# A mixture-of-experts layer on one core: two experts' first-layer rows loaded one block at a time, GpSimd's router sums ahead of two weight combinations, and the logits' additions split off

## The chip, the cores and the metric

The kernel runs on one core of a Trainium2 chip. A core has TensorE (PE, matrix products into the eight PSUM banks), VectorE (DVE, elementwise work and reductions), ScalarE (ACT, activations and copies), GpSimd (POOL, elementwise work in SBUF and its own DMA queue) and SyncE (SP, here only a DMA queue). The engines run side by side, each takes its instructions in program order, and they wait for one another on semaphores. The time is the device time of one execution, in microseconds (us). Before the change it is 463.31 us, the median of three runs (463.06 to 463.71).

## The reference

For 8 sequences of 512 tokens with 256 features each, all in float32:

```
nx       = layer_norm(x)
weights  = softmax(nx Wq (ctx Wk)^T / 16)          # 64 context rows per sequence
evidence = weights (ctx Wv)
combined = [nx, evidence, cond]                    # 768 features
probs    = softmax(combined router_W + router_b)   # 3 experts
h_e      = silu(combined e_w1[e] + e_b1[e])        # 512 wide, e = 0, 1, 2
routed   = sum_e probs_e (h_e e_w2[e] + e_b2[e])
g        = sigmoid(silu(combined gate_w1 + gate_b1) gate_w2 + gate_b2)
out      = x + g (routed out_w + out_b)
```

## The kernel before

**Pairs and products.** The sequences are worked on two at a time, so there are four pairs j = 0 to 3. Matrix products over a pair are done with seven products instead of eight, so weights and activations are first combined by a few subtractions and additions. `combine_weights(g)` does this for expert g's first layer (g = 3, that is E, is the gate): four GpSimd instructions (L248 to L251) read the first two blocks of the weight tile `w1`, write sums into `ws`, and one of them (L250) writes back into `w1`. `combine_gate` does the same for the gate's second layer.

**Weights.** `load_first(g, part)` loads 256 rows of expert g's first weights into `w1`, as two blocks of 128 rows, with one DMA on SP's queue. Part 0 (the rows for nx) of experts 1 and 2 is issued late, after the anchors' rows. The tile `w1` holds its four blocks one behind the other in each partition, each block with the columns of all three experts and the gate, so one expert's two blocks are two stretches with other experts' columns between them.

**The first pair.** The setup is part of the run, and the first pair has its own list of slots, `SLOTS_0`. In each slot two half products (64 of 128 rows each) run side by side on TensorE; after the bar stand the steps that other engines do, in the order in which they are issued. All engines follow program order here. A step `k` copies a partial sum out of PSUM (ACT), `a` and `w11.0` add one (DVE, L878), `s` is the silu (ACT, L872). `lp0.0` to `lp1.3` are `router_part`: a multiply with a running sum over one quarter of a sequence (DVE, L636), and after a sequence's fourth one, eight small GpSimd copies (L643) that spread the sums into the logits' tile `lg`. `c2` is `combine_weights(2)` and `cg` is `combine_gate`. `rl` is `router_logits`: two products with their sums (L749, L752), then four small operations on `lg` (L755 to L761). `rx` is the exponential (ACT, with a table load on both sides), `r` the normalisation and the spreading of the probabilities by DMA, `g0` a subtraction for the gate (L1222), `st` the layer norm's statistics of the next pair (L579, L580), `lx`, `l1` and `l2` loads of the next pair's x and of second-layer weights. `weigh_chunk` (L915, L912) multiplies the hidden values by the probabilities. After the slots come six units of second-layer weights (`transpose_second` on DVE, L531; `second_layer` on TensorE, L541).

**Before the slots.** `end_softmax` issues on GpSimd, in this order: `combine_weights(0)`, `router_column` (which makes `gg`, the vector of `router_part`; L414, L415), the DMAs of the router's bias and rows (L419, L435), `combine_weights(1)`. `end_setup` ends with `second_bias`, four small DVE operations on `b2o` (L562 to L567), which is read only in `outputs`.

**The pairs after.** Pairs 1 to 3 use the list `SLOTS`; their router is worked in `outputs` of the pair before.

Of the kernel before, what the change touches and what calls it, by code (L numbers as in the profile page):

```python
# [8 lines left out]
F32 = mybir.dt.float32  # L9
# [7 lines left out]
def kernel(  # L17
# [51 lines left out]
    nc = tc.nc  # L69
# [87 lines left out]
    def rows_of(w):  # L157
        return w.rearrange("(k p) n -> p k n", p=P)
# [74 lines left out]
    def load_first(g, part):  # L233
        src, n = (e_w1[g], RH) if g < E else (gate_w1, H)
        lo = part * KH
        nc.sync.dma_start(
            w1[:, lo : lo + KH, g * RH : g * RH + n], rows_of(src[part * H : (part + 1) * H, :])
        )

    def load_anchor(g):  # L240
        src = e_w1[g] if g < E else gate_w1
# [499 lines left out]
                w[side(i, h), 1 - h, :, :].rearrange("p j c -> p (j c)"),  # L741
            )

    def router_logits(j):
        w, lg, vr = S["w", j], S["lg", j], S["vr", j]
        le = work.tile([P, ED, NJ], F32, tag="le", name=f"le_{j}")
        for e in range(ED):
            pv = work.tile([P, 2, NJ, TB], F32, tag="pv", name=f"pv_{j}_{e}", bufs=1)
            nc.vector.tensor_tensor(  # L749
                pv, w, vr[:, e, :, :].unsqueeze(2).to_broadcast([P, 2, NJ, TB]), ALU.mult  # L750
            )
            nc.vector.tensor_reduce(  # L752
                le[:, e, :], pv.rearrange("p g j c -> p j g c"), AX.XY, ALU.add
            )
        nc.vector.tensor_tensor(  # L755
            lg[:, 1:, :], lg[:, 1:, :], rbias[:, j, :].unsqueeze(2).to_broadcast([P, ED, NJ]), ALU.add
        )
        nc.vector.tensor_tensor(lg[:, 1:, :], le, lg[:, 1:, :], ALU.add)
        mx = work.tile([P, NJ], F32, tag="rmx", name=f"rmx_{j}")
        nc.vector.tensor_reduce(mx, lg.rearrange("p e j -> p j e"), AX.X, ALU.max)  # L760
        nc.vector.tensor_tensor(  # L761
            lg, lg, mx.unsqueeze(1).to_broadcast([P, E, NJ]), ALU.subtract
        )

    def router_exp(j):
        S["ex", j] = work.tile([P, E, NJ], F32, tag="ex", name=f"ex_{j}")
        nc.scalar.activation(S["ex", j], S.pop(("lg", j)), AF.Exp)
# [149 lines left out]
    def gate_layer(j, steps):  # L917
# [101 lines left out]
        "P1.3 P1.1 | lp0.0 a10.0",  # L1019
        "Y.0 W.0 | k00.1 lp0.1 s10.0 lp0.2",  # L1020
        "P2.1 P1.3 | w11.0",
        "P4.0 P5.1 | a00.0 k00.3 s11.0 lp0.3 c2",
        "P6.1 P2.1 | lp1.0 s00.0 lp1.1",
        "P5.1 Z.2 | a00.1",
        "U.0 P6.1 | lp1.2 k11.1 lp1.3 cg lx l1 l2 s00.1",
        "P1.2 P5.2 | rl k10.1",
        "Y.2 P4.0 |",
        "P5.2 P1.2 | s01.0",
        "P2.3 P3.1 | k00.2 k11.2",
        "P7.1 V.1 | g0 rx",  # L1030
        "P2.2 Z.3 | st0.0 st0.1",
        "P6.2 P7.1 | st0.2 st0.3",
# [57 lines left out]
    def half_layers(j):  # L1090
# [23 lines left out]
        def half(token, k):  # L1114
# [17 lines left out]
            "xb0": lambda: load_x_blocks(2 * j),  # L1132
            "xb1": lambda: load_x_blocks(2 * j + 1),
            **{f"g{n}": lambda n=n: gate_differences(j, (n,)) for n in range(4)},
            "rl": lambda: router_logits(j),
            "rx": lambda: router_exp(j),
            "c2": lambda: combine_weights(2),
            "cg": lambda: combine_gate(),
            "lx": lambda: [load_x(b) for b in (2, 3)],
# [277 lines left out]
    with tc.manual_schedule(engines=None):  # L1417
        ctx_rows = context.flatten_outer_dims().rearrange("(t p) d -> p t d", p=P)
        for d in range(2):
            half = slice(d * NX // 2, (d + 1) * NX // 2)  # L1420
            nc.sync.dma_start(ctx_sb[:, half, :], ctx_rows[:, half, :])
        for w_sb, w in ((wk_sb, Wk), (wq_sb, Wq)):
            nc.scalar.dma_start(w_sb, rows_of(w))
        for dst, src in late_rows:
            nc.scalar.dma_start(dst, src)
        nc.sync.dma_start(wv_sb, rows_of(Wv))
        load_table(AF.Sqrt)
        load_x(0)
        load_x(1)
        load_first(E, 1)  # L1430
        load_first(E, 0)
        load_anchor(E)
        load_first(0, 1)
        load_first(0, 0)
        load_first(1, 1)
        load_first(2, 1)
        load_anchor(0)

        wake(7)
        context_transposes()  # L1440
        transpose_weights(wkT, wk_sb, "wk")
        transpose_weights(wqT, wq_sb, "wq")
        statistics(0, 0, NT)
        deviation(0, 0)
        normalize(0)
        project(wv_sb, ctxT, keep_v, "v", (0,))
        join_keys()
        project(wv_sb, ctxT, keep_v, "v", (1,))
        statistics(1, 0, NT // 2)
        small_transposes()  # L1450
        statistics(1, NT // 2, NT)
        combine_weights(E)
        transpose_x(0)
        late_scratch()
        load_anchor(1)
        load_anchor(2)
        nc.sync.dma_start(ow_sb, rows_of(out_w))
        load_first(1, 0)
        load_first(2, 0)
        nc.sync.dma_start(gw2_sb, rows_of(gate_w2))  # L1460
        load_second(0)
        deviation(0, 1)
        load_router_column()
        normalize(1)
        project(wkqT, ctxT, keep_m, "m")
        transpose_x(1)
        value_weights(0, E)
        router_anchor()
        anchor_rows(E)
        store_router_rows(0)  # L1470
        store_router_anchor()
        load_table(AF.Exp)
        combine_x(0, nc.vector, (0, 1))
        spares(6, 4, 5, 7)
        scores(0)

        def begin_softmax():
            exponents(0)
            combine_x(0, nc.vector, (2,))

        def end_softmax():
            sum_weights(0)
            softmax(0)
            nc.gpsimd.tensor_copy(wake_t, S["w", 0][:, 0, 0, 0:1])
            value_differences(0, 0)
            turn_weights(0)
            anchor_columns(E)
            combine_x(0, nc.vector, (3,))
            combine_weights(0)
            router_column()  # L1490
            spread_router_bias()
            spread_router_rows(0)
            combine_weights(1)

        def end_setup():
            value_differences(0, 1)
            late_anchors()
            for g in range(E):
                anchor_columns(g)
            value_differences(0, 2)  # L1500
            second_bias()

        for j in range(NP):


            within, between = {}, {}

            def put(where, n, step, *args):
                where.setdefault(n, []).append(lambda: step(*args))

            spares(7, 5)
            if j == 0:
                spares(4, 5, 7)
                copies = []

                def value_product(g):
                    value_weights(0, g, lambda *args: copies.append(args), False)

                def copy_values():
                    nc.scalar.copy(*copies.pop(0))  # L1520

                put(within, 1, value_product, 0)
                put(within, 1, begin_softmax)
                put(within, 5, copy_values)
                put(within, 6, load_table, AF.Silu)
                put(within, 3, value_product, 1)
                put(within, 3, copy_values)
                put(within, "sums", end_softmax)
                put(within, 7, value_product, 2)
                put(within, 7, copy_values)  # L1530
                put(within, 7, end_setup)
            else:
                put(within, 3, value_weights, j, 1, nc.scalar.copy, False)
            if j + 1 < NP:
                b0, b1 = 2 * j + 2, 2 * j + 3
                if j + 2 < NP:
                    put(between, "begin", load_x, b0 + 2)
                    put(between, "begin", load_x, b1 + 2)
                put(between, "begin", transpose_blocks, b0)
                put(between, "gate", regroup_x, b1)  # L1540
                put(between, "begin", value_weights, j + 1, E)
                put(between, "begin", store_router_rows, j + 1)
                put(between, "begin", spread_router_rows, j + 1)
                put(between, "P5", transpose_blocks, b1)
                put(between, "P6", value_weights, j + 1, 2)
                put(between, "P2", scores, j + 1)
                put(between, "P2", exponents, j + 1)
                put(between, "P2", combine_x, j + 1, nc.gpsimd)
                put(between, "P7", softmax, j + 1)
                put(between, "P7", value_weights, j + 1, 0)  # L1550
                put(between, "P7", router_logits, j + 1)
                put(between, "P3", turn_weights, j + 1)
                put(between, "P3", router_exp, j + 1)
            gate_layer(j, within)
            half_layers(j)
            outputs(j, between)

# [33 lines left out]
```

## Time and profile before

| | |
|---|---|
| median of three runs | 463.31 us (463.06 to 463.71) |
| profiled execution, its time | 463.15 us |
| profiled execution, its span | 460.8 us (granted clock 0.991) |
| PE busy | 452.3 us (98%) |
| DVE busy | 364.4 us (79%) |
| ACT busy | 214.1 us (46%) |
| POOL busy | 99.5 us (22%) |
| DMA moved | 35.31 MB, mean 77 GB/s |

The span is what the trace covers; the profiled execution's time is 2.3 us longer. Times "at 50.1" below are microseconds from the start of the span. A row of the timeline gives start, duration, engine, line, operation and tiles, and in brackets how long the engine had been idle before it and what released it. In a table of windows each engine's busy time in a stretch is given, then PEclk, the granted share of TensorE's clock. The first pair's slots run from 33.2 to 89.1, its second-layer units from 89.1 to 99.6.

### The profile page before, as it was taken

How to read it: one execution, taken by the hardware profiler on the slowest of the kernel's cores; microseconds unless marked ns; L12 is line 12 of the kernel's file. 1: busy time of each engine (PE TensorE's matmuls, PEld its weight loads, DVE VectorE, ACT ScalarE, POOL GpSimd, SP SyncE). 2: the span in 40 equal slices, each digit the busy share in tenths (PEclk: the TensorE clock that was granted, in tenths of full speed). 3: DMA queues.
4: the chain of work that ended last, by engine and by line, in shares of the span. 5: the costliest groups of instructions: out<-in, count | busy, mean ns of one | idle time of the engine just before them, and what ended most of it. 6: DMA issues, size and time to landing. Idle time of an engine off the chain costs nothing.

```text
span 460.8 us, 5500 instructions
## 1 busy us (share of the span) xinstructions
PE 452.3 (98%) x1797; PEld 217.2 (47%) x1797; DVE 364.4 (79%) x683; ACT 214.1 (46%) x373; POOL 99.5 (22%) x148
## 2 busy tenths in 40 slices
PE   9999699999999999999999999999999999999996
PEld 7544355574444444444444444444444444444445
DVE  2879699967779999578869999678969846677983
ACT  3545485457220476468220476558130456558000
POOL 5429600081053400001044300001044300000010
PEclk9999899999999999999999999999999999999999
DMA  8983664362011368402011357202011381000014
GB/s 265 384 165 92 110 195 80 48 137 46 7 23 23 47 216 133 111 0 46 8 23 23 47 189 143 37 0 46 7 23 23 47 208 23 1 0 0 1 16 75
DMA packets 119348, 35.31 MB, mean 77 GB/s; under 512 B 105981, under 2 KB 116281, under 8 KB 118809
## 3 DMA queue, kind: packets, MB, share of 16 engines
q1 hardware_dynamic: 115312, 27.02, 28.9%
q0 software_dynamic: 2080, 7.16, 4.6%
q10 hardware_dynamic: 1928, 0.80, 0.7%
q8 instruction: 14, 0.23, 0.2%
q14 instruction: 14, 0.11, 0.1%
HBM read 27.56 MB, written 7.39 MB: 76 GB/s over the span
## 4 chain that ended last, share of the span: by engine, by line
PE 87%; DMA 6%; POOL 3%; DVE 1%; issue 1%; SPq 0%; DVEq 0%; POOLq 0%
PE ps_u L836 42%; PE ps_z L836 19%; PE ps_y L836 12%; DMA w<-in_L_xcond_e_w_dram 5%; PE ps_vw L811 4%; PE ps_gu L836 3%; PE ps_w2o L541 2%; PE ps_gz L836 1%; DMA x<-in_x_dram 1%; PE ps_s L685 1%; PE ps_tokens L836 1%; POOL lg L643 1%; PE ps_gy L836 1%; POOL ws L249 1%; POOL ws L248 0%
## 5 line engine op out<-in xcount | busy, mean ns | idle before, releaser
L836 PE MATMUL ps_u<-nxT,w 64*128 64x512 f32 (+1 forms) x208 | 97.4, 595 | 0.0
L915 DVE TENSOR_TENSOR h<-h,pb 128x512 f32<-128x512 f32 x96 | 64.3, 701 | 16.2 <-ACT h L872 12.5
L836 PE MATMUL ps_u<-h,w2o 128*128 128x512 f32 x144 | 64.2, 595 | 0.0
L872 ACT ACTIVATE h<-h,abias 128x512 f32<-128x512 f32 x72 | 49.3, 718 | 29.4 <-DVE h L878 29.4
L836 PE MATMUL ps_y<-nxT,w 64*128 64x512 f32 (+1 forms) x104 | 53.3, 609 | 0.0
L836 PE MATMUL ps_z<-nxT,ws 64*128 64x512 f32 (+1 forms) x104 | 53.1, 599 | 0.0
L836 PE MATMUL ps_z<-wT,vw 64*128 64x512 f32 x104 | 52.3, 590 | 0.0
L836 PE MATMUL ps_z<-T,ws 64*128 64x512 f32 (+1 forms) x104 | 50.5, 589 | 0.0
L836 PEld LDWEIGHTS ps_u<-nxT,w 64*128 64x128 f32 (+1 forms) x208 | 37.6, 190 | 26.4 <-issue 23.8
L1322 POOL TENSOR_TENSOR yb<-yb,xb 128x512 f32<-128x512 f32 x14 | 17.7, 1266 | 148.8 <-DVE yb L1321 131.7
L836 PE MATMUL ps_u<-T,ws 64*128 64x512 f32 (+1 forms) x104 | 49.5, 598 | 0.0
L836 PE MATMUL ps_u<-T,w 64*128 64x512 f32 x112 | 48.5, 589 | 0.0
L836 PE MATMUL ps_z<-h,w2s 128*128 128x512 f32 x96 | 42.5, 592 | 0.0
L836 PEld LDWEIGHTS ps_u<-h,w2o 128*128 128x128 f32 x144 | 27.0, 190 | 32.6 <-issue 30.8
L881 ACT COPY h<-ps_u 128x512 f32<-128x512 f32 x48 | 27.7, 580 | 24.9 <-PE ps_u L836 24.9
L1289 DVE TENSOR_TENSOR h<-h,h 128x1024 f32<-128x1024 f32 x24 | 34.3, 1486 | 0.0
L836 PE MATMUL ps_u<-wT,vw 64*128 64x512 f32 x56 | 29.1, 609 | 3.8 <-DVE h L878 3.8
L427 POOL DMA_DIRECT2D vrd<-vw x8 | 5.0, 628 | 114.2 <-ACT vw L818 111.6
L836 PEld LDWEIGHTS ps_z<-h,w2s 128*128 128x128 f32 x96 | 18.2, 190 | 22.9 <-issue 22.2
L836 PE MATMUL ps_y<-wT,vw 64*128 64x512 f32 x56 | 28.3, 595 | 0.0
L811 PE MATMUL ps_vw<-w,vT 128*128 128x512 f32 (+1 forms) x64 | 26.7, 539 | 0.0
L836 PEld LDWEIGHTS ps_z<-nxT,ws 64*128 64x128 f32 (+1 forms) x104 | 19.9, 192 | 13.4 <-issue 10.8
(230 smaller groups left out, 822.2 us busy)
## 6 DMA issues: line engine op xcount, KB each, us to landing
pb<-pd POOLq DMA_DIRECT2D x4, 1536.0 KB, 6.6
xb<-in_x_dram SPq DMA_DIRECT2D x64, 64.0 KB, 2.5
out_dram<-yb SPq DMA_DIRECT2D x56, 64.0 KB, 2.0
w<-in_L_xcond_e_w_dram SPq DMA_DIRECT2D x6, 512.0 KB, 11.8
x<-in_x_dram SPq DMA_DIRECT2D x24, 128.0 KB, 3.0
xd<-x SPq DMA_DIRECT2D x24, 128.0 KB, 2.4
xg<-xd SPq DMA_DIRECT2D x48, 64.0 KB, 2.3
scr_wa<-in_L_xcond_e_w_dram SPq DMA_DIRECT2D x3, 512.0 KB, 9.3
```

What stands on the lines that cost most here:

```text
L249: add(s2, s1, a11, ALU.subtract)
L427: nc.gpsimd.dma_start(S["vrd", j][i].rearrange("e c -> c e"), S["vw", j][row_half(i), R0:])
L541: nc.tensor.matmul(ps[:, d * H : (d + 1) * H], w2["T"][u % 2][:, c : c + P], ow_sb[:, k, :], start=(k == 0), stop=(k == KH - 1),)
L643: nc.gpsimd.tensor_copy(lg[side(a, h), 2, q::NT], sums[q * TB : (q + 1) * TB, 2 * h : 2 * h + 2])
L685: nc.tensor.matmul(ps[side(i, h), g * NH : (g + 1) * NH], mr[:, k, 2 * j + i, g * TB : (g + 1) * TB], S["nxT", 2 * j + i][:, k, h * NH : ( ...
L811: nc.tensor.matmul(ps, vT[:, k, j * 2 * CT : (j + 1) * 2 * CT], w1[:, KH + k, n0:n1], start=(k == 0), stop=(k == KH - 1),)
L836: return nc.tensor.matmul(ps, lhsT, rhs, start=start, stop=True, skip_group_check=not start)
L872: nc.scalar.activation(h, h if src is None else src, AF.Silu, bias=abias[:, c, 2 * j + i : 2 * j + i + 1])
L881: nc.scalar.copy(chunk(n, i, d), part)
L915: nc.vector.tensor_tensor(h, h, S["pb", j][:, i, :, 2 * q // RC, :], ALU.mult)
L1289: nc.vector.tensor_tensor(d, p, m, ALU.subtract)
L1322: nc.gpsimd.tensor_tensor(yb, yb, S["xb", 2 * j + row][:, i, :], ALU.add)
```

## The change

Four things are changed, all of which touch the first pair alone in what runs when:

- `load_first` loads part 0 of experts 1 and 2 with two DMAs, one for each block of 128 rows, instead of one. SP's queue has two DMAs more (265 instead of 263).
- In `SLOTS_0`, `c2` goes from the sixth slot to the ninth, behind `lp1.3`, `l1` and `l2`, and `cg` goes behind it. On GpSimd the eight copies of the second sequence now stand before `combine_weights(2)`; the two combinations follow each other.
- `router_logits` is split. `evidence_logits` (the step `rl`, where it was) holds the two products with their sums. `router_logits` (the step `rs`) holds the four small operations on `lg`, three slots later, behind `k11.2`. For the later pairs the two are issued one behind the other, as before.
- `second_bias` leaves `end_setup` and becomes the step `b2`, two slots ahead of `rs`.

```diff
     def load_first(g, part):
         src, n = (e_w1[g], RH) if g < E else (gate_w1, H)
         lo = part * KH
-        nc.sync.dma_start(
-            w1[:, lo : lo + KH, g * RH : g * RH + n], rows_of(src[part * H : (part + 1) * H, :])
-        )
+        for k in range(KH) if g in (1, 2) and not part else (slice(0, KH),):
+            nc.sync.dma_start(
+                w1[:, lo : lo + KH, g * RH : g * RH + n][:, k],
+                rows_of(src[part * H : (part + 1) * H, :])[:, k],
+            )
...
-    def router_logits(j):
-        w, lg, vr = S["w", j], S["lg", j], S["vr", j]
-        le = work.tile([P, ED, NJ], F32, tag="le", name=f"le_{j}")
+    def evidence_logits(j):
+        w, vr = S["w", j], S["vr", j]
+        S["le", j] = le = work.tile([P, ED, NJ], F32, tag="le", name=f"le_{j}")
         for e in range(ED):
...
+
+    def router_logits(j):
+        lg, le = S["lg", j], S.pop(("le", j))
         nc.vector.tensor_tensor(
             lg[:, 1:, :], lg[:, 1:, :], rbias[:, j, :].unsqueeze(2).to_broadcast([P, ED, NJ]), ALU.add
         )
...
-        "P4.0 P5.1 | a00.0 k00.3 s11.0 lp0.3 c2",
+        "P4.0 P5.1 | a00.0 k00.3 s11.0 lp0.3",
         "P6.1 P2.1 | lp1.0 s00.0 lp1.1",
         "P5.1 Z.2 | a00.1",
-        "U.0 P6.1 | lp1.2 k11.1 lp1.3 cg lx l1 l2 s00.1",
+        "U.0 P6.1 | lp1.2 k11.1 lp1.3 lx l1 l2 c2 cg s00.1",
         "P1.2 P5.2 | rl k10.1",
-        "Y.2 P4.0 |",
+        "Y.2 P4.0 | b2",
         "P5.2 P1.2 | s01.0",
-        "P2.3 P3.1 | k00.2 k11.2",
+        "P2.3 P3.1 | k00.2 k11.2 rs",
         "P7.1 V.1 | g0 rx",
...
-            "rl": lambda: router_logits(j),
+            "rl": lambda: evidence_logits(j),
+            "rs": lambda: router_logits(j),
             "rx": lambda: router_exp(j),
+            "b2": lambda: second_bias(),
...
             value_differences(0, 2)
-            second_bias()
...
+                put(between, "P7", evidence_logits, j + 1)
                 put(between, "P7", router_logits, j + 1)
```

## The prediction

> **What bounds the kernel now.** I read the engines' shares first, then the page's 40 slices.
>
> ```profile
> PE 452.3 (98%) x1797; PEld 217.2 (47%) x1797; DVE 364.4 (79%) x683; ACT 214.1 (46%) x373; POOL 99.5 (22%) x148
> PE   9999699999999999999999999999999999999996
> DVE  2879699967779999578869999678969846677983
> PEclk9999899999999999999999999999999999999999
> ```
>
> TensorE is the bound in 38 of 40 slices. Only the fifth slice (46.1 to 57.6 us) has a hole in its middle, and there the granted clock dips too; the last slice is the drain at the end. So a change to the first pair is worth what it does to that hole. Next, who waits for whom, on PE and on DVE:
>
> ```profile
> PE ps_u L836 <- DVE h L878: 3.8, 1, 3.8
> DVE lg L755 <- POOL lg L643: 3.0, 1, 3.0
> ```
>
> PE waits once, 3.8 us, for an addition on DVE; shortly before, DVE waits 3.0 us for GpSimd's router copies. The chain that ended last gives the links in time (start, length):
>
> ```profile
> 15.45 16.69 DMA w<-in_L_xcond_e_w_dram
> 32.29 0.64 POOL ws L248
> 44.84 0.65 POOL ws L248
> 49.71 0.19 DVE lg L755
> 53.72 0.70 DVE h L878
> 54.46 1.22 PE ps_u L836
> ```
>
> GpSimd is held until a weight DMA lands at 32.14, is then busy without a break, finishes the second sequence's copies at 49.7, DVE does its logits, one gate subtraction (L1222) and four statistics, then `a11.1` (53.72), which releases PE. GpSimd's own timeline shows the queue:
>
> ```profile
> 32.29 0.63 POOL L248 TENSOR_TENSOR ws<-w 128x256 f32<-128x256 f32 x1 [5.70 <-DMA w<-in_L_xcond_e_w_dram]
> 41.98 2.78 POOL L643 COPY lg<-ls 32x2 f32<-32x2 f32 x8
> 47.25 0.63 POOL L251 TENSOR_TENSOR ws<-w,ws 128x256 f32<-128x256 f32 x1
> 47.95 1.73 POOL L643 COPY lg<-ls 32x2 f32<-32x2 f32 x8
> ```
>
> The windows add the second half of the loss (after the stretch: its length, then each engine's busy time, then the clock):
>
> ```profile
> 49.70:54.40 4.70, 0.98 (x6) 0.15 (x2) 4.25 (x15) 2.79 (x3) 2.27 (x4) 0.85 0.75 120
> 54.40:60.00 5.60, 5.54 (x14) 2.87 (x16) 5.36 (x18) 4.16 (x7) 2.70 (x6) 0.51 0.16 24
> 70.00:80.00 10.00, 10.00 (x49) 5.26 (x47) 9.86 (x28) 5.57 (x9) 0.00 (x0) 1.00 0.40 69
> ```
>
> After the hole PE runs at half clock. Half products, 0.43 us apart before, follow at 0.86 us from 54.46 to 59.74: 5.3 us for 2.65 us of work. The hole itself is 3.95 us (next start due at 50.51, came at 54.46). Together 6.6 us of PE's time. In the third window DVE is the full engine: what DVE has gained by 54 us limits what PE can keep.
>
> **The change, part by part.** The sum is made against the profiled execution: 463.15 us, span 460.8, 2.3 around it; it lies 0.16 under the median of 463.31.
>
> *Block loads.* Expert 0's combination reads columns of `w1`, which one load of experts 1 or 2, seen as a stretch from its first to its last column, spans. In the built order its first instruction waits for two of SP's DMA lanes before, and for one after; the lane left is also that of expert 0's own load, issued at 8.5 and landed by 15.4. So GpSimd need not wait until 32.14 but starts behind `wake_t` at 26.6, 5.7 us earlier. Then 2.7 us for expert 0, 1.6 for `gg`, 2.1 for four DMA issues, 3.4 for expert 1 (its blocks landed by 30.3 as one load, wanted now at 33.1): free at about 36.4, before 42.0. The four block DMAs carry the same bytes in the same place; the two more issues, 0.47 us each, are hidden in SP's idle time between 35.3 and 40.7, ahead of the x loads, whose start DVE sets. Without that cover: 0.9 us on x, which lands at 44.9 now and is read at 48.
>
> *Copies ahead of the combinations.* The second sequence's copies need only DVE's last `lp1.3`, about 42.4 in the new order, so they end about 43.8. DVE reaches the logits at about 46.5. Its 2.97 us wait is gone. What is late next: `combine_weights(2)` ends about 46.7, 1.2 us before its 47.9, so being put behind costs nothing; PE's first reader of those sums, P6.6, comes ten slots behind the hole, at about 59. The gate's combination ends about 49 instead of 52.1, read at 99.6.
>
> *`second_bias` and the split.* The four `b2o` operations (1.18 us from 36.07 to 37.25) move behind the evidence sums. They still stand ahead of `a11.1`, so its chain does not get shorter; the `lp` steps get 1.2 us earlier. The split moves four small operations (1.0 us) three slots on. Both cost nothing more; neither removes work.
>
> *DVE's chain.* From 33.38 to `a11.1` at 53.72 are 20.34 us, with 2.97 us of waiting. The same instructions stand in it afterwards: 33.38 + 17.37 = 50.75. Durations shift where GpSimd moves:
>
> ```profile
> 40.70 0.83 DVE L636 SCALAR_TENSOR_TENSOR junk<-x,gg 128x256 f32<-128x256 f32 x1
> 41.57 0.74 DVE L636 SCALAR_TENSOR_TENSOR junk<-x,gg 128x256 f32<-128x256 f32 x1
> 43.33 0.43 DVE L636 SCALAR_TENSOR_TENSOR junk<-x,gg 128x256 f32<-128x256 f32 x1
> ```
>
> The same operation takes 0.42 to 0.45 elsewhere, 0.83 and 0.74 beside expert 1's combination. That one will now lie over 33.1 to 36.4, on the bias additions (already 0.39 to 0.68 beside expert 0's) and the first `lp`. Two junks give back 0.70, one takes 0.35: `a11.1` starts at 50.4, ends 51.1, PE goes on at 51.15 instead of 50.51. A rest of 0.65 us stays.
>
> The rule that speaks against the change is in the Trainium skill, page SBUF — State Buffer, section "SBUF: two separate sides": VectorE and GpSimd share a port pair as an exclusive lock, and a VectorE operation with two SBUF inputs blocks fully against a GpSimd one. The 0.83 agrees. By it each such operation could lose a whole GpSimd instruction, which would put the time near the slow rival's below.
>
> *The clock.* It went to half about 53.0 (0.85 in 49.7 to 54.4 makes 1.4 us at half), 2.3 us after the last product ended. A rest of 0.65 is far below, so I count the 2.65 as gone. Bounds: 0 and 2.65 back.
>
> The Trainium skill, TensorE: Matmul & The Clock Gate, Part 1, has the clock halved after an idle window of about 3.4 us that runs freely. By that a rest up to 3.4 would be safe where the row says 2.3; the forecast is the same by both.
>
> *Sum.* PE at 60: 3.95 - 0.65 + 2.65 = 5.95 us earlier. But DVE is only 53.72 - 50.40 = 3.3 us earlier, and full to 98. Its waits between 54 and 98 are 0.8 for ACT (stays) and 0.2, 0.2 and 0.3 for PE and a DMA that come earlier (0.17 + 0.18 + 0.27 in the rows: 0.6 gone). The last turn of second-layer weights ends at 97.65 and PE reads it at 97.85: 0.15 of slack. PE keeps 3.3 + 0.6 + 0.15 = 4.05 us, and gives 1.9 back in small waits between 75 and 98. Behind 100 all is shifted alike: 463.15 - 4.05 = 459.1, **459.1 us**.
>
> **The rivals.**
>
> *No locks on DVE's chain (chance 0.18).* The bias additions (0.39, 0.68, 0.65) fall to about 0.2 each, `b2o` (0.60, 0.30) to 0.2 each, the junks to 0.42. That takes 1.1 + 0.5 + 0.35 off: `a11.1` at 48.4, no hole. DVE 5.3 + 0.75 earlier, PE at most 6.6: 457.1. For it: GpSimd is idle between its copies. Against: combinations lie beside both groups again.
>
> *A longer rest (0.18).* The logits and `g0` are slowed by the combinations, `a11.1` at 52.3, rest 2.5: DVE 1.4 + 0.75 gives 461.0; if the clock falls too, PE keeps 1.4: 461.8.
>
> *The block loads release nothing (0.05).* GpSimd starts at 32.29 still. `gg` ends at 36.64, so the first `lp` waits 0.6; the copies, now ahead, end about 46.5, with DVE. Lead 2.5, gain 3.3: 459.9.
>
> *Slower (0.05).* The two combinations that now follow each other, eight instructions and 5.4 us on GpSimd, lie over DVE's evidence, bias, logits and `g0` (43.5 to 49). If DVE is locked out for their whole length on top of the durations used, `a11.1` starts at 55.8, 2.1 late: 465.2. It turns from gain to loss at 3.3 us of lock. Against: beside these instructions the logits (0.18 to 0.32) and `g0` (0.68) were measured already.
>
> *Nothing (0.02).* Another DVE operation waits as long.
>
> **How the numbers follow.** The forecast has 0.52. The range 457.2 to 461.3 holds it, the release rival, two thirds of the first and half of the second, 0.78 to 0.82. A measurement here tells 0.2% (0.9 us) from nothing. Faster than 462.4: forecast, first rival, release rival and nearly all of the longer rest, 0.92; within 0.2%: 0.03; slower: 0.05.
>
> **What would show it.** In the changed trace GpSimd's L250 (then the first line of a combination) should start near 26.6 and no DVE wait for L645 be left; the DVE addition before PE's hole near 50.4; the hole under 1 us; PEclk 1.00 throughout 50 to 60; new PE waits for DVE, 0.1 to 0.5 us each, between 75 and 96, on the transposes (L533) above all. I am wrong if x lands after 48 (st waits for DMA), if the clock falls after a hole under 2 us, or if DVE rows of the logits and bias grow past 0.7 us.

## The result, and the profile after

The changed kernel takes 461.33 us (median of 8 runs, 460.99 to 461.83); the kernel before, run beside it on the same chip, takes 463.51 us (8 runs, 462.17 to 464.19). The ratio is 0.9956, with an interval of 0.9943 to 0.9969: faster by 2.0 us, between 1.4 and 2.6. The prediction had 459.1, a gain of about 4. The direction was right and half of the gain is missing.

The profiled execution took 461.67 us, its span is 459.3. In it a load of `Wv` at the very start landed later, and everything up to the first-layer bias begins 0.75 us later than in the trace before (`ar_blocks` at 34.13 instead of 33.38). The change doesn't touch that load, and with the new block loads alone (experiment 1) `ar_blocks` starts at 33.45; so wherever a time of this trace is held against the trace before, 0.75 is taken off: the span says 1.5 us, the pair itself gained 2.25.

The page, engines and slices:

```profile
PE 451.5 (98%) x1797; PEld 216.6 (47%) x1797; DVE 364.0 (79%) x683; ACT 214.1 (47%) x373; POOL 100.7 (22%) x148
PE   8999989999999999999999999999999999999996
PEclk9999999999999999999999999999999999999999
```

The hole in the fifth slice has shrunk and no slice shows a lower clock. A new dent stands in the sixth slice. The waits between 33 and 100 us say where (engine, line, what it waited for: us in total, times, longest):

```profile
DVE h L920 <- DMA pb<-pd: 1.8, 1, 1.8
PE ps_z L841 <- DVE h L883: 1.3, 1, 1.3
PE ps_u L841 <- DVE h L883: 1.1, 1, 1.1
```

and before, for the transfer (GpSimd's issue, DVE's first product with it):

```profile
59.21 0.56 POOL L795 DMA_DIRECT2D pb<-pd  x1 [1.70 <-DMA pd<-prT]
65.62 0.69 DVE L915 TENSOR_TENSOR h<-h,pb 128x512 f32<-128x512 f32 x1 [0.17 <-DMA pb<-pd]
```

The 3.8 us before U.1 (the product that `a11.1` releases) are now 1.1, and DVE's 3.0 us for GpSimd's copies are gone. In their place DVE waits 1.8 us for `pb`, the transfer that brings the first pair's probabilities to all partitions, and PE waits 1.3 us behind DVE. The windows (length, busy time of PE, PEld, DVE, ACT and POOL, clock, DMA share, GB/s):

```profile
49.70:54.40 4.70, 3.65 (x18) 1.33 (x14) 4.23 (x17) 3.17 (x5) 1.32 (x4) 1.00 0.73 116
54.40:60.00 5.60, 5.60 (x27) 2.82 (x27) 5.46 (x15) 5.50 (x9) 1.82 (x5) 1.00 0.32 88
65.00:70.00 5.00, 3.66 (x19) 2.09 (x20) 4.98 (x9) 2.96 (x5) 0.00 (x0) 1.00 0.73 176
```

The clock is 1.00 throughout, so the half-speed stretch of before is gone. GpSimd's timeline (start, length, line; idle time before it in brackets):

```profile
27.31 0.63 POOL L250 TENSOR_TENSOR ws<-w 128x256 f32<-128x256 f32 x1
40.30 4.72 POOL L645 COPY lg<-ls 32x2 f32<-32x2 f32 x12 [0.91 <-DVE junk L638]
45.11 0.64 POOL L250 TENSOR_TENSOR ws<-w 128x256 f32<-128x256 f32 x1
45.82 0.72 POOL L251 TENSOR_TENSOR ws<-ws,w 128x256 f32<-128x256 f32 x1
46.50 0.72 POOL L252 TENSOR_TENSOR w<-w 128x256 f32<-128x256 f32 x1
47.19 0.64 POOL L253 TENSOR_TENSOR ws<-w,ws 128x256 f32<-128x256 f32 x1
```

The first combination starts 5.7 us earlier than before (27.31 less 0.75 against 32.29), the copies are through at 45.0, and expert 2's combination follows them. Beside exactly that combination DVE now runs `second_bias`:

```profile
45.39 0.38 DVE L564 COPY b2o<-ar_blocks 128x6 f32<-128x6 f32 x1
45.81 1.44 DVE L566 TENSOR_SCALAR b2o<-b2o 128x2 f32<-128x2 f32 x2
47.28 0.55 DVE L569 TENSOR_TENSOR b2o<-b2o,cols 128x2 f32<-128x2 f32 x1
```

Four operations on 128x2 and 128x6 take from 45.39 to 47.83, and in the records each ends 0.02 to 0.03 us behind the end of one of GpSimd's four (45.74, 46.54, 47.22, 47.82). In the kernel before the same four took 0.60, 0.43 for two, and 0.16:

```profile
36.07 0.60 DVE L562 COPY b2o<-ar_blocks 128x6 f32<-128x6 f32 x1
36.71 0.43 DVE L564 TENSOR_SCALAR b2o<-b2o 128x2 f32<-128x2 f32 x2
37.17 0.16 DVE L567 TENSOR_TENSOR b2o<-b2o,cols 128x2 f32<-128x2 f32 x1
```

The chain of waits after (start, length):

```profile
51.74 0.69 DVE h L883
53.52 1.51 POOL pd L796 x3
55.03 1.58 DMA pd<-prT
57.27 7.73 DMA pb<-pd
65.63 0.69 DVE h L883
66.36 0.69 PE ps_z L841
```

From `a11.1` at 51.74 the chain goes through the probabilities' four small stores, the transfer to all partitions with 7.7 us, and `a10.3`, which stands on DVE's queue behind the first product with `pb` (`w00.1`). Before, that transfer was issued at 59.21 and there 6.4 us later, and DVE waited 0.2 us for it. It is now issued 1.94 us earlier in trace time and arrives only 0.6 us earlier.

The same DVE instruction in both traces, before less after plus 0.75, gives the lead along the way: 2.73 us at `a11.1`, 3.0 at 63, 1.35 at the first product with `pb` and until 87, and 2.2 from 99 to the end. PE leads by about 5 us at 63, by about 3 from 70 to 85, and by 2.2 from 99 on.

### The profile page after: what moved, and what is told of

Same layout as the page of the kernel before. It is cut to its first block, busy times and chain, and to the rows that moved or that the text cites. A ratio compares the mean times of both kernels' runs of the same rounds, so it can differ in the third digit from the quotient of the medians.

```text
span 459.3 us, 5502 instructions
## 1 busy us (share of the span) xinstructions
PE 451.5 (98%) x1797; PEld 216.6 (47%) x1797; DVE 364.0 (79%) x683; ACT 214.1 (47%) x373; POOL 100.7 (22%) x148
## 4 chain that ended last, share of the span: by engine, by line
PE 90%; DMA 4%; DVE 3%; SPq 1%; issue 1%; POOL 0%; DVEq 0%; POOLq 0%
PE ps_u L841 40%; PE ps_z L841 19%; PE ps_y L841 12%; PE ps_vw L816 5%; PE ps_gu L841 3%; PE ps_w2o L543 2%; DMA pb<-pd 2%; PE ps_s L687 2%; PE ps_gz L841 1%; DMA scr_w<-in_L_xcond_Wv_dram 1%; PE ps_tokens L841 1%; PE ps_v L352 1%; PE ps_m L352 1%; PE ps_gy L841 1%; DVE junk L638 1%
## 5 line engine op out<-in xcount | busy, mean ns | idle before, releaser
L841 PE MATMUL ps_z<-T,ws 64*128 64x512 f32 (+1 forms) x104 | 51.6, 591 | 0.0
L841 PE MATMUL ps_y<-nxT,w 64*128 64x512 f32 (+1 forms) x104 | 51.5, 590 | 0.0
L841 PEld LDWEIGHTS ps_y<-nxT,w 64*128 64x128 f32 (+1 forms) x104 | 19.4, 187 | 13.6 <-issue 13.4
```

The costliest lines, as they stand in the source:

```text
L841: return nc.tensor.matmul(ps, lhsT, rhs, start=start, stop=True, skip_group_check=not start)
```

## The experiments

Two theories. *Place*: what is missing was lost by what DVE has to wait for or stand beside in the new order, namely `b2o` beside the combination, and the transfer. *Early start*: only GpSimd's early start matters and the new order is worth nothing. For the transfer, three causes were open: the stores of x that run beside it, GpSimd's queue, or something else. Every ratio below is against the kernel before, run beside it on the same chip. Each trace is one execution, and they begin differently, as above; so hold `a11.1` against `ar_blocks` of the same trace: it starts 20.3 us later before the change, 17.6 after it, and 18.1, 17.4, 16.2 and 15.8 in experiments 1, 2, 3 and 5.

**1. The block loads alone** (the kernel before, with the new `load_first`)

```diff
-        nc.sync.dma_start(
-            w1[:, lo : lo + KH, g * RH : g * RH + n], rows_of(src[part * H : (part + 1) * H, :])
-        )
+        for k in range(KH) if g in (1, 2) and not part else (slice(0, KH),):
+            nc.sync.dma_start(
...
```

> Only the block loads; steps, copies and bias stand as before. If the block loads are what frees GpSimd, its first combination after the wake copy starts near 27 instead of 32.3. The second sequence's copies still stand behind the third expert's combination: combination from about 42, copies to 46.5 to 48. Theory 'order of the copies matters most': DVE still waits 1 to 2 us, PE's hole stays over 2 us, 462 to 463.4. Theory 'the early start is enough': no DVE wait, hole 1 us, 461.3 like the whole change. If the load does not matter: GpSimd starts at 32 still and 463.3.

Measured: 461.66 us, ratio 0.9949 (0.9937 to 0.9961). GpSimd starts at 26.62; DVE still waits 0.9 us for the copies; `a11.1` at 51.50; PE waits 1.5 us at U.1 and 1.6 at the transfer, which takes 8.0 us. The block loads alone give as much as the whole change.

**2. The order alone** (the changed kernel with the old loads)

```diff
-        for k in range(KH) if g in (1, 2) and not part else (slice(0, KH),):
-            nc.sync.dma_start(
...
+        nc.sync.dma_start(
+            w1[:, lo : lo + KH, g * RH : g * RH + n], rows_of(src[part * H : (part + 1) * H, :])
+        )
```

> The whole change without the block loads (one load each for the second and third expert). GpSimd should start at 32.3 again, so the first router sum waits about 1 us for gg; DVE's addition a11.1 comes about 1.2 us later than with the whole change (51.7), the hole is about 2.4 us. Theory 'the transfer of the probabilities sets the end of the stretch': it lands 0.6 to 1.2 us later too, time 461.9 to 462.6. Theory 'DVE's full queue alone': the same 1.2 us, 462.5. If the block loads are worth nothing: 461.3.

Measured: 462.07 us, ratio 0.9971 (0.9953 to 0.9989), from 12 runs between 460.89 and 465.90; the trace is of the fastest of them. GpSimd starts at 32.21 and is late with everything; expert 2's combination begins only at 46.66, so that the same `b2o` operations lie beside copies instead:

```profile
46.05 0.16 DVE L562 COPY b2o<-ar_blocks 128x6 f32<-128x6 f32 x1
46.25 0.36 DVE L564 TENSOR_SCALAR b2o<-b2o 128x2 f32<-128x2 f32 x2
46.65 0.16 DVE L567 TENSOR_TENSOR b2o<-b2o,cols 128x2 f32<-128x2 f32 x1
```

0.7 us instead of 2.4, in the same place of DVE's queue. `a11.1` comes at 51.12, 17.4 us behind `ar_blocks` against 17.6 in the changed kernel, although GpSimd starts 5 us later. So the two parts are not additive: the early start pulls expert 2's combination onto `b2o`.

**3. `second_bias` back in the setup** (the rest of the change kept)

```diff
-        "Y.2 P4.0 | b2",
+        "Y.2 P4.0 |",
...
             value_differences(0, 2)
+            second_bias()
```

> The whole change, but second_bias back in end_setup. In the changed kernel its four operations took 2.37 us beside GpSimd's combination, 1.18 before. Theory 'the move cost what the lock added': they take 1.0 to 1.4, a11.1 starts near 50.6, the hole nearly closes, the probabilities come 1.1 us earlier and the time is 460.2. Rival 'they only change places with the router sums' (then slowed in their stead): a11.1 stays at 51.7 and 461.3.

Measured: 459.78 us, ratio 0.9908 (0.9895 to 0.9921), better than the changed kernel, and the two intervals don't overlap. `a11.1` at 49.48, no PE wait at U.1; left are 1.4 us of DVE for the transfer (6.6 us this time) and 0.9 of PE behind it. Against experiment 1 it differs by the order of copies, combinations and logits alone: 0.9949 goes to 0.9908. "Early start is enough" falls: the order is worth another 1.9 us, and the moved `second_bias` hid that.

**4. The stores of x out of the transfer's way**

```diff
-        "P2.4 P7.2 | g3 k10.3 nm0.0 k00.6",
...
-        "P3.3 P1.4 | nm1.3 xd1 xg w00.1 k00.5",
+        "P3.3 P1.4 | w00.1 nm0.0 nm0.1 nm0.2 nm0.3 xd0 nm1.0 nm1.1 nm1.2 nm1.3 xd1 xg k00.5",
```

> The whole change, but DVE normalises the next pair's x, and SP stores it, only after the first product with the probabilities, so no store of x lies beside the transfer of the probabilities (pb). Theory 'the stores slow the transfer': issue to landing 6.4 us, as before the change, not 7.7. Rival 'it is slower for another reason' (GpSimd's descriptors beside DVE, its earlier start): 7.7 again. The time itself gets worse, since DVE has no work left in the wait: hole 3.3 to 4.6 us there, 465 to 467.

Measured: 467.26 us in one run (464.16 before). PE waits 4.6 us, since normalization now stands behind DVE's wait, and the time says nothing about the question. The transfer does: 8.0 us from issue to landing, with no store of x beside it. The stores are not the cause.

What is, the packets show. The transfer is 128 packets of 12,288 bytes on 16 DMA engines. Below, from the packet records of the twelve traces (the last six are told of further down): start of the first packet, end of the last one on 15 of the engines, end on the 16th, start of the one 16 KB packet of the queue that loads instructions near that time, and issue to landing. All in us.

```
                              first   15 done  16 done  instr.  landing
before                        60.46   65.2     65.3     65.53   6.4
after                         58.53   63.4     64.5     62.18   7.7
1 blocks only                 58.80   63.3     64.5     62.16   8.0
2 order only                  57.88   62.7     64.0     60.74   7.9
3 bias back                   56.99   61.8     62.0     56.63   6.6
4 stores late                 58.53   63.2     64.5     62.15   8.0
5 bias late                   56.70   61.5     62.3     58.64   7.4
6 weigh behind                57.37   62.5     63.9     61.55   8.2
7 spread by SP                56.93   61.7     61.8     61.42   6.2
8 bias back, weigh behind     57.41   62.2     62.3     56.99   6.5
9 bias back, spread by SP     57.08   62.1     63.3     60.49   7.7
10 all                        57.37   62.4     63.5     61.14   7.6
```

The records name no engine: packets are counted to one engine where the next starts as the last one ends, which gives 16 chains. Fifteen engines always take 4.5 to 5.2 us. One takes 0.85 to 1.34 us longer wherever the instruction packet (0.9 us long) starts well inside the transfer. In each of these eight traces a packet of just this chain ends within 0.01 us of the start of the instruction packet, and the chain's next one starts as that packet ends (experiment 9: up to 60.49, instructions 60.49 to 61.42, on from 61.41). In the traces where it starts before the first packet (3 and 8), after the last (before), or 0.4 us before the end (7, when one engine is done with its last packet at 61.42), there is no such engine. The profile shows the packet in the DMA view of the transfer's own window (queue, packets, MB, share of 16 engines); after, 58.5 to 64.5:

```profile
q0 software_dynamic: 143, 1.57, 74.6%
q1 hardware_dynamic: 241, 0.23, 15.4%
q8 instruction: 1, 0.02, 0.9%
```

and before, 60.4 to 65.4, without it:

```profile
q0 software_dynamic: 144, 1.57, 83.9%
q1 hardware_dynamic: 75, 0.08, 5.5%
```

**5. `second_bias` behind `a11.1`**

```diff
-        "Y.2 P4.0 | b2",
+        "Y.2 P4.0 |",
...
-        "P3.2 P2.3 | a00.2 dev",
+        "P3.2 P2.3 | a00.2 dev b2",
```

> The changed kernel with second_bias moved on DVE's queue from the place ahead of a11.1 to behind it, beside deviation, where GpSimd has no combination to run. Theory (the five small operations cost DVE 2.4 us only because GpSimd's combine(2) runs beside them, 45.1 to 47.8, and because they stand ahead of a11.1): a11.1 near 49.4 instead of 51.74, the five together 0.7 us as in the run with the order alone (0.16, 0.36, 0.16), the probabilities' transfer issued near 55, and a time of 459.3 to 460.2, as with second_bias back at its old place (459.78). Rival (it is the number of operations ahead of the router that counts, not their place beside combine(2)): they would take about as long at the new place, a00.2 comes 1 to 2 us late and the time stays at 460.8 to 461.5.

Measured: 459.65 us, ratio 0.9908 (0.9892 to 0.9925). `a11.1` at 49.15, and `b2o` from 53.91 to 54.66, with GpSimd idle:

```profile
53.91 0.17 DVE L564 COPY b2o<-ar_blocks 128x6 f32<-128x6 f32 x1
54.11 0.36 DVE L566 TENSOR_SCALAR b2o<-b2o 128x2 f32<-128x2 f32 x2
54.50 0.16 DVE L569 TENSOR_TENSOR b2o<-b2o,cols 128x2 f32<-128x2 f32 x1
```

As *place* has it (the operations that the expectation counts as five are these four). The transfer took 7.4 us here, with the packet inside, so the gain over the changed kernel is that of `b2o` and not of the packet.

With `b2o` gone, the logits lie beside the same combination:

```profile
45.01 0.38 DVE L760 TENSOR_TENSOR lg<-lg,rbias 128x16 f32<-128x16 f32 x1
45.42 0.17 DVE L763 TENSOR_TENSOR lg<-le,lg 128x16 f32<-128x16 f32 x1
45.63 0.18 DVE L765 TENSOR_REDUCE rmx<-lg 128x8 f32<-128x24 f32 x1
45.84 0.38 DVE L766 TENSOR_TENSOR lg<-lg,rmx 128x24 f32<-128x24 f32 x1
46.15 0.68 DVE L1229 TENSOR_TENSOR hg<-hg,hg 128x512 f32<-128x512 f32 x1
46.15 1.27 POOL L252 TENSOR_TENSOR w<-w 128x256 f32<-128x256 f32 x1
```

Two of them end with an instruction of GpSimd's (45.36, 46.19), the others don't, and beside `g0` it is GpSimd that takes longer, 1.27 us instead of 0.72. The four take 1.2 us, against 1.05 in the changed kernel. So the place alone doesn't set the cost; what decides which of the two engines waits, no run here separates.

**6. `a10.3` ahead of the first product with `pb`**

```diff
-        "P3.3 P1.4 | nm1.3 xd1 xg w00.1 k00.5",
-        "P6.6 Z.6 | a10.3 k00.4",
+        "P3.3 P1.4 | nm1.3 xd1 xg k00.5",
+        "P6.6 Z.6 | a10.3 w00.1 k00.4",
```

> The changed kernel with one step of DVE's queue exchanged: the addition a10.3 ahead of the first multiplication by the probabilities (w00.1), which waits for their transfer. Theory (the transfer lands 7.7 us after its issue instead of 6.4, DVE waits 1.8 us for it, and PE's 1.34 us come only from a10.3 standing behind that wait): a10.3 at 63.2, no PE wait at 65, and the time 0.7 to 1.3 us less, 460.0 to 460.6. Rival (DVE's 1.8 us are what counts, whatever stands behind them): the next addition, a11.3, is then late by as much, a new PE wait of about 1 us appears near 67 and the time stays within 0.3 us of 461.33.

Measured: 460.95 us, ratio 0.9934 (0.9915 to 0.9953). The PE wait on `ps_z` at 65 is gone, but PE waits twice for DVE on `ps_u`, 1.6 us together, and DVE still waits 1.7 us for the transfer. The interval overlaps that of the changed kernel: by the times neither theory is decided, and the trace lies between them.

**7. The first pair's probabilities half by SP**

```diff
-            nc.gpsimd.dma_start(
+            (nc.gpsimd if j or q % 2 else nc.sync).dma_start(
                 pd[q].rearrange("(n c) -> n c", c=TB), prT[q * TB : q * TB + n, :]
             )
...
-        nc.gpsimd.dma_start(
+        (nc.gpsimd if j else nc.sync).dma_start(
             S["pb", j].rearrange("p i h e t -> p (i h) (e t)"), pd.partition_broadcast(P)
         )
```

> The changed kernel, first pair alone: two of the four small stores of the probabilities and the transfer back to all partitions are issued by SP instead of GpSimd. The stores land about 0.9 us earlier, so the transfer is issued near 56.3 instead of 57.27. Theory (in the runs so far 15 of the 16 DMA engines took 4.9 us for their part, and one took 1.1 us more where a 16 KB packet of the instruction queue ran on it between the first and the last packet; in the kernel before that packet came 0.2 us after the end): the transfer's packets still take 4.9 us, 6 to 6.3 us from issue to the last but one engine, and 7 to 7.5 us to the landing if the instruction packet again falls inside it; DVE's wait falls from 1.8 to about 1 us, the PE wait from 1.3 to about 0.5, and the time is 460.3 to 460.9. Rival (GpSimd's queue is slow because DVE runs beside it while the descriptors are written): on SP's queue the transfer takes 5 to 5.5 us, lands before 62, no wait is left and the time is 459.8 to 460.2.

Measured: 458.83 us, ratio 0.9889 (0.9871 to 0.9908), a larger gain than either theory gave. About 0.5 us of it lies outside the span: the time is 1.8 us longer than the span here and in experiments 9 and 10, 2.2 to 2.5 in the medians of the others; why stays open. Issued at 55.95, landed at 62.13: 6.2 us, where the packet came at 61.42, when 15 engines were 0.3 us from done. DVE has no wait for it. This trace begins with `ar_blocks` at 34.14, like the one after, so the two compare directly: the first product with `pb` comes 1.76 us earlier, the last one (94.71 against 96.47) also 1.76, and the span is 1.9 shorter. The whole of DVE's wait counts, more than the 1.3 us of PE's. That no wait for the transfer is left is the rival's sign, but its 5 to 5.5 us for the transfer didn't come; I had expected some 1 us of wait to stay. PE still waits 1.2 us at U.1, since `b2o` is beside the combination here.

**8. Experiment 3, with `a10.3` and two router sums of the next pair ahead of `w00.1`**

```diff
-        "P3.3 P1.4 | nm1.3 xd1 xg w00.1 k00.5",
-        "P6.6 Z.6 | a10.3 k00.4",
+        "P3.3 P1.4 | nm1.3 xd1 xg k00.5",
+        "P6.6 Z.6 | a10.3 lg0.0 lg0.1 w00.1 k00.4",
...
-        "P7.5 P4.3 | s00.4 lg0.0",
-        "P5.4 P5.6 | w00.4 s01.3 lg0.1",
+        "P7.5 P4.3 | s00.4",
+        "P5.4 P5.6 | w00.4 s01.3",
```

> second_bias back at its old place (459.78 us) and, with it, a10.3 and the first two of the next pair's router sums (lg0.0, lg0.1) ahead of the first multiplication by the probabilities, so that DVE has work while their transfer is on its way. Theory (the 0.9 us that PE waits at 63 in that kernel is the rest of the loss): no PE wait at 63, DVE's wait for the transfer below 0.5 us, time 458.7 to 459.2. Rival (DVE's later work sets the time, so what it waits here comes out later): 459.5 to 459.9.

Measured: 458.46 us, ratio 0.9884 (0.9865 to 0.9903), the lowest of all, 2.9 us under the changed kernel and 0.2 under the theory's range; the intervals of 7 and 10 overlap with its own. Between 33 and 100 us the waits view has no line of PE for anything, and none of DVE for the transfer. The windows of its trace:

```profile
50.00:55.00 5.00, 5.00 (x25) 2.28 (x23) 4.76 (x16) 3.75 (x6) 2.37 (x5) 1.00 0.74 115
60.00:65.00 5.00, 5.00 (x23) 1.91 (x21) 4.89 (x13) 3.08 (x6) 0.00 (x0) 1.00 0.94 319
65.00:70.00 5.00, 4.94 (x22) 2.85 (x22) 5.00 (x10) 2.26 (x5) 0.00 (x0) 1.00 0.69 122
```

PE is full where before and after had their holes.

**9 and 10. Experiments 3 and 7 together, and with the order of 8** (no other edit)

> second_bias back at its old place, and the first pair's probabilities stored and spread half by SP as in the run before (458.83 us with second_bias at its new place). Theory (two separate losses: five small operations that take 2.37 us beside GpSimd's combine(2), and DVE's wait for the transfer, after which DVE's own work sets the time until 97): a11.1 near 49.5, the transfer issued near 54.2 and landed 6.2 to 6.5 us later, near 60.5, ahead of DVE, which comes to its first product near 61; no DVE wait for it and no PE wait there. The time is 459.78 less the 1.4 us of DVE's wait: 458.2 to 458.6. Rival (the two share one loss, and either cure is enough): 458.7 to 459.2, no better than with SP alone.

> The last run with a10.3, lg0.0 and lg0.1 ahead of the first product with the probabilities too. Theory: with the transfer there before DVE wants it, the exchange has nothing left to hide, and the time is within 0.3 us of the run without it (458.2 to 458.6). Rival (an addition that PE waits for gains from being earlier in any case): 457.6 to 458.1.

Measured: 459.54 us, ratio 0.9904 (0.9889 to 0.9920), and 458.78 us, ratio 0.9891 (0.9875 to 0.9907). Both miss. In 9 the stores were ready earlier, but SP was still issuing second-layer weights and took them up only at 53.92; the transfer was issued at 56.09, not 54.2, and with the packet inside it took 7.7 us (first DVE's wait for it, then PE's behind that):

```profile
DVE h L920 <- DMA pb<-pd: 2.1, 1, 2.1
PE ps_z L841 <- DVE h L883: 1.6, 1, 1.6
```

In 10 the same transfer is late, 7.6 us, and the order with work ahead of `w00.1` hides all but 0.5 us of it. The two runs also settle the question of the queue: on SP's queue the transfer takes 6.2 us without the packet inside and 7.6 or 7.7 with it, on GpSimd's 6.4 to 6.6 and 7.4 to 8.2.

## Why the prediction was half right

*Block loads*: right in the start, expected at 26.6, measured at 27.31 less 0.75. Behind it GpSimd waited 1.26 us for the DMA of the router's bias (`rbd`), which the prediction didn't count, so it was through with expert 1's combination at 37.65 (same scale) and not at 36.4.

*Copies ahead of the combinations*: right. No DVE wait for GpSimd's copies (L645) is left; the copies end at 44.3 (same scale), the prediction had 43.8.

*`second_bias` and the split*: this step failed. "Both cost nothing more" priced the four operations at their old 1.18 us. By the prediction's own times their new place lies beside `combine_weights(2)`: that was put at 43.8 to 46.7, and DVE was to reach the logits, right behind them, at 46.5. They took 2.4 us. Experiments 2 and 5 show the cause, since the same four take 0.7 us beside copies or beside nothing, and experiment 5 its worth, 0.9956 to 0.9908; experiment 3 has the same ratio, but there the packet also lay outside the transfer. The prediction's own sign, rows of "the logits and bias" past 0.7 us, came: two of the four took 1.44. The prediction had quoted the rule of the lock and applied it to the rows that it had, not to the instructions that the change moves. The Trainium skill, SBUF — State Buffer, section "Who interferes with whom", names `copy` and `tensor_scalar`, besides a `tensor_tensor` with two SBUF inputs, as operations that can contend with GpSimd; the rows agree, 0.38, 1.44 for two, and 0.55 against 0.16, 0.36 for two, and 0.16 in experiment 2.

*DVE's chain*: 17.0 us predicted, 17.61 measured, so `a11.1` leads by 2.73 us instead of 3.3. `b2o` added 1.2; the bias additions and the operation on `vw` behind them gave back 0.7 (0.44 and 0.80 against 1.56 and 0.42); the first `lp` operations took 0.84 and 0.74 beside expert 1's combination, so the junks gave back nothing where 0.35 was counted. The rest before U.1 is 1.1 us instead of 0.65.

*The clock*: right. PE's wait of 1.1 us left it at 1.00, and so did those of 1.6 us in experiments 1 and 9.

*Sum*: the second failed step is the term "0.2, 0.2 and 0.3 for PE and a DMA that come earlier (0.17 + 0.18 + 0.27 in the rows: 0.6 gone)". One of these waits was that for `pb`. It did not go but grew to 1.8 us. The transfer could be issued only behind `a11.1` and four stores, 2.7 us earlier, when DVE came 3.0 us earlier; with the 6.4 us of before, the wait would have been 0.5. The other 1.3 us are the transfer's longer time. DVE's lead fell from 2.73 to 1.35 there. Behind it the small waits of before did go, and the lead grew to 2.2. So of the 1.8 us missing from 4.05, 0.6 are `a11.1`, 1.4 the transfer, less 0.2. And PE gave back about 2 us at that one place and some 0.8 more until 99, where the prediction had 1.9 "in small waits between 75 and 98".

*The rivals*: the release rival was wrong in its mechanism (the blocks do release) and the longer rest too high at 2.5. The slower rival had the right place, the combinations over "DVE's evidence, bias, logits and `g0`"; but of these the four bias operations alone got slower, 1.2 us and not the 3.3 from which it decides. The logits (0.16 to 0.32) and `g0` (0.68), beside the gate's combination as before, kept their times. The rival without locks, 457.1, failed on the rows of `b2o`.

## What to carry to other kernels

When a step moves to another place of its engine's queue, price it by what the other engines will run beside it there, in the new order's times; small operations are no exception, for each can take as long as the large one beside it. When a whole stage moves forward, look for transfers whose issue moves less than their reader, and put the reader behind work that does not need them: with three steps of it DVE's wait fell to nothing and to 0.5 us (experiments 8 and 10; one step alone, in 6, left 1.7), where shortening the transfer's path (7 and 9) depended on what the queue was doing.

## What was not expected of the hardware

A load of instructions can delay a data transfer by its own length. One 16 KB packet of about 0.9 us stood in line on one of 16 DMA engines, that engine was done 0.85 to 1.34 us behind the others, and the 1.5 MB transfer landed 7.4 to 8.2 us after its issue instead of 6.2 to 6.6, in eight of twelve traces (in 1 and 4 its first packet was also 0.3 to 0.5 us later). Ahead of the transfer's packets (3 and 8) it made no engine late at the end. That it lay inside in those eight and outside in four is read from the records, one execution of each kernel; no run moved the packet alone, and which engine's program it brings, and what asks for it, stays open.

The delay was not GpSimd's queue. The Trainium skill, SBUF — State Buffer, section "SBUF: two separate sides", describes transfers issued by GpSimd that VectorE holds up and that a queue of another kind cures; here SP's queue had the same late engine, 7.6 and 7.7 us.
